# The next expert's first transposes between two experts' bodies, and layer 0's neighbour sums in three segments

## The chip, the cores and the metric

The kernel runs on one core of a Trainium2 chip. A core has five engines with a sequence of instructions each: TensorE (PE in the profile) multiplies matrices and transposes, VectorE (DVE) and ScalarE (ACT) work element by element, GpSimd (POOL) issues the transfers that gather and scatter by an index, and SyncE (SP) issues most other transfers. They wait for each other through semaphores. The metric is the time on the device in microseconds (us): the median over runs of the whole program.

## The reference

The input x has 625 rows (nodes) of 1024 float32 values, and 10,625 edges (src, dst). Two parts are added to it in turn:

```python
deg_inv = 1.0 / maximum(degree(dst), 1)
def sage(h, W_self, W_neigh, b):
    mean = segment_sum(h[src], dst) * deg_inv
    return h @ W_self + mean @ W_neigh + b
x = x + sage(relu(sage(layernorm(x), ...layer 0)), ...layer 1)

n = layernorm(x)
w = softmax(n @ gate_w.T) kept for each row's two largest of 8 experts, else 0
for each expert e:
    g, u = n @ gate_up[e].T          # 1408 values each
    out += w[:, e] * ((silu(g) * u) @ down[e].T)
out += sigmoid(n @ shared_expert_gate_w.T) * (shared expert of 176 values)
x = x + out
```

## The kernel before

**Graph part.** The edges are counted into an adjacency matrix on the chip, so that a neighbour sum is a matrix product. Layer 0's neighbour sums are added to h1T, the transposed hidden rows, in the region "sum0": for each half of the nodes (313 and 312 columns) and for each of 8 chunks of 128 features, PE makes a sum in PSUM bank (4 + c) mod 8 (p_sum), and DVE scales it, adds it to h1T and applies the relu, three instructions. Layer 1 begins with `plain(0, half, wn1, q)` (L955): the products p_y of the first 125 nodes into banks 6 and 7. The products of the other nodes follow, by blocks.

**Experts.** The 8 experts run one after the other. An expert's tokens, at most 512, are gathered by their index into four tiles of 128 rows (rows), transposed by PE into xg (features on the partitions, tokens along the free axis) and multiplied by the gate/up weights wg in 11 chunks; silu and the product with u give ht; the down products by wd follow, each scaled by the token's weight gw into ys, and POOL scatters ys onto the output with an add.

The number of tokens of an expert is known only while the kernel runs. The code of an expert therefore is a region with several bodies, one for each number of 64-token units, n = 0 to 7, and every engine branches into the body that fits (Rec.emit, L294: a Switch); PE has further variants for the width. For n up to 2 a body is small: `few` for 128 tokens, with the tokens as the stationary operand, `unit` for 64 left over. Above that it is `many`, with the weights stationary. Ahead of the branch stands a hint (`hint`, L727), which tells the sequencer where it will go. A body ends with a branch to the code behind the region, which is common to all: the hint for the next expert, the copies gw (`weights`, L1307, DVE) and the branch into the next expert's body.

Each body is cut into segments (`k.point()`): three for gate/up (s = 0, 1, 2), then one for each part of the down products. An instruction outside a region, or a DMA issued within it, that needs something of a segment waits for the end of that segment on the engine concerned, since the bodies differ within it. A wait from outside on an earlier instruction of a segment is so a wait on the segment's last one.

**Around the change.** `expand(j, ...)` (L1303) transposes token tile j: for each of two groups of four features' chunks, PE makes four transposes into one PSUM bank and an engine copies the bank into xg; its `engines` name the two that copy, DVE and ACT if nothing is said. `expand(0, ...)` for the next expert stands at the end of the last gate/up segment (L1569), ahead of the down products; tiles 1 to 3 are made at the start of the expert's own body (L1555), copied by ACT. Program order is queue order on each engine. The first expert's tile 0 is made ahead of its region (L1321). In `many` the first chunk of gate/up products is done in two halves over the features, so that its first half needs only the first of the two copies; `few` and `unit` do it in one piece. The gathers of the next expert's rows are issued by POOL after an expert's first gate/up segment. The weights of the next expert are loaded into wg and wd by SP as the products that read them end.

Of the kernel before, what the change touches and what calls it, by code (L numbers as in the profile page):

```python
# [301 lines left out]
def gnn_moe(nc, x, src, dst, w_gnn0, w_gnn1, b0, b1, w_gu, w_down, ws_up, ws_down, out):  # L302
# [203 lines left out]
    def tt(o, a, b, op):  # L506
        return k.op("DVE", lambda h: h.tensor_tensor(o, a, b, op), r=[a, b], w=[o])  # L507
# [382 lines left out]


    k.open("sum0", 2)
    for n, (n0, nn) in enumerate(HALVES):
        for k.cls in range(2):
            for c in range(KD):
                q, o, t = bank("p_sum", (4 + c) % 8)[:, :nn], node_half(c, n), summed[c % 2][:, :nn]
                cols = slice(c * 128, (c + 1) * 128)
                if k.cls:
                    mm(q, [(y0[:, s, cols], at[:, s, n0:n0 + nn]) for s in range(NT)])
                    add(o, q)  # L900
                else:
                    mm(q, [(z[:, s, cols], cb[:, s, n0:n0 + nn]) for s in range(NT) for z in (zh, zm, zl)])
                    tt(t, q, deg_row[:, n0:n0 + nn], ALU.mult)
                    add(o, t)
                ts(o, o, 0.0, None, ALU.max)
        k.cls = None
        k.point()
# [395 lines left out]
    def expand(j, m=128, two=(4, 5), engines=("DVE", "ACT")):  # L1303

        transpose(xg[:, :, j * 128:j * 128 + m], rows[j][:, :D], m, two, "p_xg" if two[0] > 3 else "p_gu", engines)

    def weights(e):  # L1307
        for j in range(NTL):
            copy(gw[:, e % 2, j:j + 1], rows[j][:, D + e:D + e + 1])
# [75 lines left out]
    def gu_bank():  # L1385
        bank_turn[0] = (bank_turn[0] + 1) % 4
        return bank("p_gu", bank_turn[0])

    def gu_banks():
        gu_bank()  # L1390
        b = bank_turn[0]
        gu_bank()
        return b, bank_turn[0]

    def gate(h, q):

        act(h, q[:, :, 0, :], AF.Silu)
        tt(h, h, q[:, :, 1, :], ALU.mult)

    def few(s):  # L1400

        for c in range(4 * s, min(4 * s + 4, FC), 2):
            n = min(2, FC - c)
            q = gu_bank().rearrange("p (c a i) -> p c a i", c=2, a=2)[:, :n]
            mm_all(q.rearrange("p c a i -> p c (a i)"),
                   [(xg[:, i, :128], wg[:, c:c + n, i].rearrange("p c a i -> p c (a i)")) for i in range(KD)])
            gate(hid[:, c:c + n, :], q)

    def few_transpose(s, b, eng):
# [8 lines left out]
        k.op("PE", fn, r=[h, ident], w=[p])  # L1418
        copy(ht[:, 4 * s:4 * s + n, :128], p, eng)

    def side_by_side(jobs):

        def fn(h, m=None):
            for n in range(len(jobs[0][1])):
                for o, pairs in jobs:
                    got = h.matmul(o, *pairs[n], start=n == 0, stop=n == len(pairs) - 1, skip_group_check=True)  # L1426
            return got
        k.op("PE", fn, r=[x for o, pairs in jobs for p in pairs for x in p], w=[o for o, pairs in jobs])

    def unit(s, t0):  # L1430

        q = gu_bank().rearrange("p (c a i) -> p c a i", c=2, a=2)
        x = [xg[:, i, t0:t0 + 64] for i in range(KD)]

        def job(half, to, what):
            return q[64 * half:64 * half + 64][:, to], [(x[i], what(i)) for i in range(KD)]
        c = 4 * s
        if c + 4 <= FC:
            side_by_side([(q[64 * b:64 * b + 64].rearrange("p c a i -> p c (a i)"),
                           [(x[i], wg[:, c + 2 * b:c + 2 * b + 2, i].rearrange("p c a i -> p c (a i)"))  # L1440
                            for i in range(KD)]) for b in range(2)])
            gate(hid_u[:, 2 * s:2 * s + 2, :], q)
        else:

            side_by_side([(q[64 * b:64 * b + 64, 0].rearrange("p a i -> p (a i)"),
                           [(x[i], wg[:, c + b, i].rearrange("p a i -> p (a i)")) for i in range(KD)]) for b in range(2)])
            side_by_side([(q[64 * b:64 * b + 64, 1, 0, :],
                           [(x[i], wg[:, c + 2, i, 1 - b]) for i in range(KD)]) for b in range(2)])
            gate(hid_u[:, 2 * s:2 * s + 1, :], q[:, :1])
            o = hid_u[:64, 2 * s + 1, :]  # L1450
            act(o, q[64:, 1, 0, :], AF.Silu)
            tt(o, o, q[:64, 1, 0, :], ALU.mult)
# [18 lines left out]
    def many(s, m):  # L1471

        for c in range(4 * s, min(4 * s + 4, FC)):
            pp = [bank("p_gu", 2 * (c % 2) + a) for a in range(2)]

            parts = (range(KD // 2), range(KD // 2, KD)) if c == 0 else (range(KD),)
            for some in parts:
                for a in range(2):
                    mm_all(pp[a], [(wg[:, c, i, a, :], xg[:, i, :]) for i in some], True, some is parts[0], some is parts[-1])
            o = ht[:, c, :m]  # L1480
            act(o, pp[0][:, :m], AF.Silu)
            tt(o, o, pp[1][:, :m], ALU.mult)
# [52 lines left out]
    for e in range(NE):  # L1535
        more = e + 1 < NE
        k.open(e, UNITS)

        def transposed(s, n):

            if n > 0:
                few_transpose(s, 4, "ACT")
            if n % 2 == 0:
                unit_transpose(s, 64 * n, 5, "ACT")

        for s in range(SEG):
            for n in range(UNITS):
                k.cls = n
                full, odd = (n + 1) // 2, n % 2 == 0
                small = n < SMALL // 64  # L1550
                if small and full:
                    few(s)
                if s == 0:
                    for j in range(1, full + odd):
                        expand(j, 128 if j < full else 64, ((4, 5), (0, 1), (2, 3))[j - 1], ("ACT", "ACT"))  # L1555
                    if odd:
                        for b in range(2):
                            copy(gs[64 * b:64 * b + 64, :], gw[:64, e % 2, full:full + 1])
                if small:
                    if odd:  # L1560
                        unit(s, 128 * full)
                    if s:
                        transposed(s - 1, n)
                else:
                    many(s, 64 * n + 64)
                if e == s == 0:
                    own_indices(range(HEAD, NE), 7, "ACT")
                if s == SEG - 1 and more:
                    expand(0, two=gu_banks() if small else (2, 3))  # L1569
            k.cls = None  # L1570
            k.point()
            if e == s == 0:
                wd_loads = [load(wd[c], w_down[0, c]) for c in range(FC)]
            if more:
                for c in range(4 * s, min(4 * s + 4, FC)):
                    load_gu(e + 1, c, [wd_loads[DOWN_FIRST]] if c == 0 else ())
                if s == 0:
                    for j in range(NTL):
                        gather(e + 1, j)
        now = []  # L1580


        for j, stages in ((None, (0, 1)), *((j, (0, 1)) for j in range(NTL - 1, 0, -1)), (0, (0,)), (0, (1,))):
            for n in range(UNITS):
                k.cls = n
                full, odd = (n + 1) // 2, n % 2 == 0
                first = n < SMALL // 64 and (j is None or not odd or full == 0)
                between = (lambda: transposed(SEG - 1, n)) if first else None
                if odd and (j is None and full or j == 0 and not full):
                    down_unit(e, 128 * full, between, stages)  # L1590
                elif j is not None and j < full:
                    down(e, j, between, odd, stages)
            k.cls = None
            k.point()
            halves_of = (None,) if more else (0, 1)
            if stages == (0,):
                if more:
                    wd_loads = [load(wd[c], w_down[e + 1, c]) for c in range(CUT)]
                continue
            for half in halves_of:  # L1600
                now.append(scatter(e, j, half))
        k.close()
        scattered = now
        if more:
            hint(e + 1, bodies)
            weights(e + 1)
            if e + 2 == NE:
                for half in range(2):
                    ts(idx_h[:, half, :], idx[:, e + 1, :], 2.0, float(half), ALU.mult, ALU.add)
            wd_loads += [load(wd[c], w_down[e + 1, c]) for c in range(CUT, FC)]  # L1610
# [111 lines left out]
```

## Time and profile before

| what | value |
|---|---|
| runs | 1119.47, 1120.13, 1117.36 us; median 1119.47 |
| the profiled execution | 1116.6 us, span 1114.8 us |
| mean granted TensorE clock | 0.991 |
| PE, busy | 1078.0 us |
| DVE, busy | 289.7 us |
| ACT, busy | 127.5 us |
| POOL, busy | 50.2 us |
| data moved | 186.53 MB, mean 167 GB/s |
| experts' part, first to last gate/up or down product | 407.86 to 1104.7 us |

In a row of the profile's timeline stand the start, the busy time, the engine, the line, the operation, output <- inputs with their shapes, the count, and in brackets how long the engine stood idle before it and what ended that idle time. "issue" is idle time that no wait in the profile explains. An engine's name with a q (DVEq) is its sequencer: it takes the branches and hints, which the busy times leave out. "p_gu", "p_xg" and "p_down" are PSUM banks under the names of their use; the transposes of a token tile appear as L597 with p_gu or p_xg, depending on the bank. The seven experts' boundaries lie at 501.9, 533.0, 736.5, 795.2, 826.3, 940.2 and 1046.8 us.

### The profile page before, as it was taken

To read this page: it belongs to the slowest core of one execution; us is meant where nothing else is said; L and a number is where in the kernel's file an instruction comes from. 1 tells how busy PE (TensorE), PEld (TensorE's weight loads), DVE (VectorE), ACT (ScalarE), POOL (GpSimd) and SP (SyncE) were. 2 spreads that over 40 slices of the span, in tenths; PEclk is the share of its full clock that TensorE was granted. 3 is DMA by queue.
4 is the path that set the end of the run, shared out by engine and by line. 5 is a ranking of instruction groups with operands and counts; after the bars stand their busy time and mean duration, and the time that the engine had idled before them with its cause. 6 is when DMAs were issued, how large, how long until landed. Compare 5 with 4: busy or idle time off the path is not lost.

```text
span 1114.8 us, 10854 instructions
## 1 busy us (share of the span) xinstructions
PE 1078.0 (97%) x4265; PEld 616.8 (55%) x4265; DVE 289.7 (26%) x719; ACT 127.5 (11%) x246; POOL 50.2 (5%) x56
## 2 busy tenths in 40 slices
PE   6999999999999989999899999999989999999996
PEld 3554777444555544544455554445349965995452
DVE  7954556653644350101000000000010000000000
ACT  1122320211000240101100000001010000000010
POOL 0000000000000040001000000100100001000001
PEclk9999999999999999999999999999999999999998
DMA  9600021311042259969933113278799545642601
GB/s 299 250 1 5 1 66 47 152 49 31 1 174 88 74 159 314 362 251 386 403 134 151 76 75 123 38 253 338 271 404 366 226 163 159 231 180 115 215 34 26
DMA packets 40874, 186.53 MB, mean 167 GB/s; under 512 B 6933, under 2 KB 6933, under 8 KB 29300
## 3 DMA queue, kind: packets, MB, share of 16 engines
q1 hardware_dynamic: 34432, 168.18, 39.1%
q0 software_dynamic: 6000, 16.26, 6.3%
q8 instruction: 62, 1.02, 0.4%
q14 instruction: 120, 0.98, 0.3%
q10 hardware_dynamic: 260, 0.09, 0.0%
HBM read 170.51 MB, written 13.99 MB: 165 GB/s over the span
## 4 chain that ended last, share of the span: by engine, by line
PE 93%; DVE 2%; issue 2%; ACT 1%; DMA 1%; SPq 0%; POOL 0%; POOLq 0%; ACTq 0%; DVEq 0%
PE p_gu L547 34%; PE p_down L1493 20%; PE p_y L539 11%; PE p_sum L539 6%; PE p_h L539 5%; PE p_sage L539 5%; PE p_gu L1426 5%; PE p_gs L539 2%; PE p_downs L539 1%; PE pa L656 1%; PE p_gu L597 1%; PE p_tr L597 1%; DVE ln_st L554 1%; DMA rows<-xfw,idx 0%; DMA xa<-in_x_dram 0%
## 5 line engine op out<-in xcount | busy, mean ns | idle before, releaser
L547 PE MATMUL p_gu<-xg,wg 128*128 128x224 f32 (+1 forms) x1056 | 264.5, 414 | 1.2 <-ACT xg L515 1.2
L547 PEld LDWEIGHTS p_gu<-xg,wg 128*128 128x128 f32 x1056 | 202.2, 192 | 62.7 <-issue 60.4
L1493 PE MATMUL p_down<-wd,ht 128*128 128x512 f32 (+1 forms) x616 | 229.5, 594 | 0.0
L1493 PEld LDWEIGHTS p_down<-wd,ht 128*128 128x128 f32 (+1 forms) x616 | 95.0, 175 | 125.0 <-issue 124.8
L507 DVE TENSOR_TENSOR ht<-ht,p_gu 128x256 f32<-128x256 f32 (+3 forms) x63 | 27.5, 437 | 369.2 <-PE p_gu L547 232.7
L547 PE MATMUL p_gu<-wg,xg 128*128 128x512 f32 (+1 forms) x288 | 116.4, 564 | 0.9 <-DVE ht L507 0.6
L547 PEld LDWEIGHTS p_gu<-wg,xg 128*128 128x128 f32 x288 | 55.0, 192 | 59.8 <-issue 57.4
L539 PE MATMUL p_y<-wn,h0T 128*125 128x512 f32 x160 | 72.7, 609 | 1.3 <-ACT h0T L515 1.3
L520 ACT ACTIVATE ht<-p_gu 128x256 f32<-128x256 f32 (+3 forms) x63 | 24.9, 396 | 427.8 <-PE p_gu L547 357.7
L1426 PE MATMUL p_gu<-wg,xg 128*64 128x512 f32 (+2 forms) x384 | 58.3, 461 | 0.5 <-ACT xg L515 0.5
L503 DVE TENSOR_SCALAR ys<-p_down,gw 128x512 f32<-128x512 f32 x10 | 7.5, 751 | 182.6 <-PE p_down L1493 182.6
L539 PE MATMUL p_h<-h0T,ws 128*128 128x313 f32 x192 | 51.1, 426 | 0.0
L539 PEld LDWEIGHTS p_y<-wn,h0T 128*125 128x125 f32 x160 | 29.9, 192 | 37.9 <-issue 35.1
L1360 POOL DMA_INDIRECT out_dram<-ys,idx x13 | 19.9, 1532 | 554.3 <-DVE ys L503 320.2
L539 PEld LDWEIGHTS p_h<-h0T,ws 128*128 128x128 f32 x192 | 36.2, 189 | 14.7 <-issue 0.4
L1426 PEld LDWEIGHTS p_gu<-wg,xg 128*64 128x64 f32 x384 | 25.5, 137 | 32.2 <-issue 28.1
L539 PE MATMUL p_y<-wn,h1T 128*125 128x512 f32 x96 | 41.6, 593 | 1.5 <-DVE h1T L503 1.5
L539 PE MATMUL p_sage<-ws,h1T 128*125 128x512 f32 x96 | 41.9, 592 | 0.0
L503 DVE TENSOR_SCALAR os<-node,src_f 125x640 f16<-125x640 f16 x85 | 33.2, 391 | 2.8 <-PE pa L656 2.8
L539 PEld LDWEIGHTS p_y<-wn,h1T 128*125 128x125 f32 x96 | 18.0, 188 | 24.5 <-issue 22.2
L539 PEld LDWEIGHTS p_sage<-ws,h1T 128*125 128x125 f32 x96 | 17.9, 188 | 22.1 <-issue 21.7
L504 DVE TENSOR_SCALAR od<-node,dmod,dval_i 125x79 bf16<-125x79 f16 x85 | 26.5, 312 | 0.0
(202 smaller groups left out, 775.9 us busy)
## 6 DMA issues: line engine op xcount, KB each, us to landing
wg<-in_w_gu_dram SPq DMA_DIRECT2D x88, 1024.0 KB, 10.8
wd<-in_w_down_dram SPq DMA_DIRECT2D x88, 512.0 KB, 9.0
wn<-in_w_gnn_dram SPq DMA_DIRECT2D x16, 512.0 KB, 13.8
ws<-in_w_gnn_dram SPq DMA_DIRECT2D x16, 512.0 KB, 13.4
xr<-in_x_dram SPq DMA_DIRECT2D x5, 448.0 KB
xfw<-xf SPq DMA_DIRECT2D x5, 448.0 KB
out_dram<-xr SPq DMA_DIRECT2D x5, 448.0 KB
xa<-in_x_dram SPq DMA_DIRECT2D x4, 448.0 KB
```

The costliest lines, as they stand in the source:

```text
L503: return k.op("DVE", lambda h: h.tensor_scalar(o, i, s1, None, op0=op0), r=aps, w=[o])
L504: return k.op("DVE", lambda h: h.tensor_scalar(o, i, s1, s2, op0=op0, op1=op1), r=aps, w=[o])
L507: return k.op("DVE", lambda h: h.tensor_tensor(o, a, b, op), r=[a, b], w=[o])
L520: return k.op("ACT", lambda h: h.activation(o, i, f, **kw), r=aps, w=[o])
L539: k.op("PE", lambda h, a=a, b=b, s=s, e=e: h.matmul(o, a, b, start=s, stop=e, skip_group_check=True), r=[a, b], w=[o])
L547: got = h.matmul(o if m is None else o[:, :m], a, b if m is None else b[:, :m], start=start and n == 0, stop=stop and n == len(pairs) - 1, ...
L554: k.op("DVE", lambda h, part=part, st=st: h.bn_stats(st, part), r=[part], w=[st])
L597: got = h.transpose(pt[:, c, :], i[:n, (4 * g + c) * 128:(4 * g + c + 1) * 128], ident[:n, :n])
L656: k.op("PE", lambda h, s=s: h.matmul(pa[:, s, :], o_s[:, s, :], o_d[:, :DIG], start=c == 0 and s == 0, stop=c == EC - 1 and s == NT - 1, s ...
L1360: h.indirect_dma_start(out=to, out_offset=bass.IndirectOffsetOnAxis(ap=i, axis=0), in_=y, in_offset=None, compute_op=ALU.add).then_inc(s, 16)
L1426: got = h.matmul(o, *pairs[n], start=n == 0, stop=n == len(pairs) - 1, skip_group_check=True)
L1493: got = h.matmul(o[job], *pairs[job][n], start=n == 0, stop=n == FC - 1, skip_group_check=True)
```

## The change

1. The transposes of the next expert's tile 0 and their two copies are taken out of the bodies (where they were between the gate/up and the down products) and stand behind the region, between the next expert's hint and its gw copies. Both copies are DVE's; before, one was DVE's and one ACT's. The banks are 4 and 5. In the large bodies the later tiles change banks for that: tile 1 uses 2 and 3 (before 4 and 5), tile 2 uses 4 and 5 (before 0 and 1), tile 3 stays at 2 and 3.
2. The first chunk of gate/up products is cut into two halves over the features in `few` and `unit` as well (first_chunk).
3. In "sum0" the second half of the nodes is two segments, chunks 0 to 3 and chunks 4 to 7, each with its end.

```diff
-    for n, (n0, nn) in enumerate(HALVES):
+    for n, some in ((0, range(KD)), (1, range(KQ)), (1, range(KQ, KD))):
+        n0, nn = HALVES[n]
         for k.cls in range(2):
-            for c in range(KD):
+            for c in some:
...
-    def gu_banks():
-        gu_bank()
-        b = bank_turn[0]
-        gu_bank()
-        return b, bank_turn[0]
...
+    def first_chunk(c):
+
+        return (range(KD // 2), range(KD // 2, KD)) if c == 0 else (range(KD),)
 
     def few(s):
...
-            mm_all(q.rearrange("p c a i -> p c (a i)"),
-                   [(xg[:, i, :128], wg[:, c:c + n, i].rearrange("p c a i -> p c (a i)")) for i in range(KD)])
+            for some in first_chunk(c):
+                mm_all(q.rearrange("p c a i -> p c (a i)"),
+                       [(xg[:, i, :128], wg[:, c:c + n, i].rearrange("p c a i -> p c (a i)")) for i in some],
+                       False, some[0] == 0, some[-1] == KD - 1)
...
-    def side_by_side(jobs):
+    def side_by_side(jobs, some=range(KD)):
 
         def fn(h, m=None):
-            for n in range(len(jobs[0][1])):
+            for n in some:
...
     def unit(s, t0):
...
+            for some in first_chunk(c):
+                side_by_side(jobs, some)
...
                     for j in range(1, full + odd):
-                        expand(j, 128 if j < full else 64, ((4, 5), (0, 1), (2, 3))[j - 1], ("ACT", "ACT"))
+                        two = (4, 5) if small or j == 2 else (2, 3)
+                        expand(j, 128 if j < full else 64, two, ("ACT", "ACT"))
...
-                if s == SEG - 1 and more:
-                    expand(0, two=gu_banks() if small else (2, 3))
...
         if more:
             hint(e + 1, bodies)
+            expand(0, engines=("DVE", "DVE"))
             weights(e + 1)
```

More of the change, by code (lines that the diff above doesn't have):

```diff
@@ L1427, in fn @@
             return got
-        k.op("PE", fn, r=[x for o, pairs in jobs for p in pairs for x in p], w=[o for o, pairs in jobs])
+        k.op("PE", fn, r=[x for o, pairs in jobs for n in some for x in pairs[n]], w=[o for o, pairs in jobs])
     def unit(s, t0):
@@ L1438, in unit @@
         if c + 4 <= FC:
-            side_by_side([(q[64 * b:64 * b + 64].rearrange("p c a i -> p c (a i)"),
-                           [(x[i], wg[:, c + 2 * b:c + 2 * b + 2, i].rearrange("p c a i -> p c (a i)"))
-                            for i in range(KD)]) for b in range(2)])
+            jobs = [(q[64 * b:64 * b + 64].rearrange("p c a i -> p c (a i)"),
+                     [(x[i], wg[:, c + 2 * b:c + 2 * b + 2, i].rearrange("p c a i -> p c (a i)"))
+                      for i in range(KD)]) for b in range(2)]
+            for some in first_chunk(c):
+                side_by_side(jobs, some)
             gate(hid_u[:, 2 * s:2 * s + 2, :], q)
@@ L1474, in many @@
             pp = [bank("p_gu", 2 * (c % 2) + a) for a in range(2)]
-            parts = (range(KD // 2), range(KD // 2, KD)) if c == 0 else (range(KD),)
-            for some in parts:
+            for some in first_chunk(c):
                 for a in range(2):
-                    mm_all(pp[a], [(wg[:, c, i, a, :], xg[:, i, :]) for i in some], True, some is parts[0], some is parts[-1])
+                    mm_all(pp[a], [(wg[:, c, i, a, :], xg[:, i, :]) for i in some], True, some[0] == 0, some[-1] == KD - 1)
             o = ht[:, c, :m]
```

## The prediction

> **What bounds the kernel now.** I read first the page's busy shares and its chain of work that ended last:
>
> ```profile
> PE 1078.0 (97%) x4265; PEld 616.8 (55%) x4265; DVE 289.7 (26%) x719; ACT 127.5 (11%) x246; POOL 50.2 (5%) x56
> PE 93%; DVE 2%; issue 2%; ACT 1%; DMA 1%; SPq 0%; POOL 0%; POOLq 0%; ACTq 0%; DVEq 0%
> ```
>
> TensorE (PE) sets the time: whatever makes it wait counts in full, and another engine's work counts only where PE waits for it. So the next view is the chain in order of time, at the seven places where one expert's body ends and the next begins:
>
> ```profile
> 521.91 0.87 PE p_gu L597 x8
> ...
> 525.11 7.88 PE p_down L1493 x36
> 532.99 3.98 issue
> 536.97 1.54 PE p_xg L597 x8
> 538.51 2.34 PE p_gu L597 x12
> ...
> 670.04 66.44 PE p_down L1493 x176
> 736.48 27.46 PE p_gu L547 x64
> ```
>
> A body's last down product ends at a time that I call E. At E = 736.48 PE goes from the last down product to the next gate/up product with no gap. The seven E are 501.93, 532.99, 736.48, 795.23, 826.28, 940.21 and 1046.82; the next gate/up product starts after 0, 8.31, 0, 0, 5.49, 1.12 and 0 us (the chain and the timeline). The 8 transposes "p_gu L597" before the down products are the ones that the change moves: 0.87 us of PE for each of 7 experts.
>
> The third view is DVE's timeline and its sequencer's records at the same boundary:
>
> ```profile
> 736.52 0.75 DVE L503 TENSOR_SCALAR ys<-p_down,gw 128x512 f32<-128x512 f32 x1 [18.13 <-PE p_down L1493]
> 742.54 0.34 DVE L516 COPY gw<-rows 128x1 f32<-128x1 f32 x4 [5.27 <-issue]
> ```
> ```profile
> L294 DVEq COMPARE_BRANCH  x2: 53/54/56, 736.5 to 742.9; - x2
> ```
> ```profile
> L727 DVEq MOVE  x3: 36/36/36, 741.9 to 742.3; - x3
> ```
>
> DVE issues its scaling of the last down product at E, then takes the branch out of the body at 736.5. Its next instruction, the first of the branch hint, comes at 741.9: 5.4 us in which it executes nothing. The hint takes some 0.6 us, and the gw copies start at 742.54. Today that lateness is free, as nothing that PE needs soon stands there. The gw copies start at E + 6.71, 6.17, 6.06, 6.20, 6.11, 6.89 and 6.02 at the seven boundaries, whichever body is left.
>
> **The change, part by part.**
>
> *Removed from the bodies.* The 8 transposes of the next expert's first tokens: 7 x 0.87 = -6.1 us on PE. They filled PE while ACT and DVE gated the last chunk. Behind them PE has the last transposes of hid only after two further down chunks (0.86 us or more, "p_down L1493" before "p_ht"), against about 0.75 us for ACT's silu (0.28) and DVE's product (0.29) with their hand-overs, so I put that cover's loss at 0; lost whole it costs at most 0.5 us in the four small bodies. ACT loses one 0.58 us copy in each, off the path.
>
> *Put between the bodies.* In the changed kernel's order DVE has: branch out, hint, two xg copies, gw copies, branch in. PE's 8 transposes come at E, 1.04 us by the timeline, and are done long before DVE comes. DVE's first copy stands where the gw copies stand now, and the row for this tile is 0.69 us ("COPY xg<-p_gu", 692 ns). PE starts about 0.04 us after the copy (as at 831.73 to 831.77 after ACT's). The next gate/up product therefore starts at E plus the gw offsets plus 0.73: 7.44, (6.90), 6.79, 6.93, 6.84, 7.62, 6.75. The second copy comes 0.69 us later, hidden by the new split of the first chunk: four products of 0.43 us, or eight in the large bodies. The cover gone, it is 0.69 us each, 5 in all.
>
> The second boundary leads into the body for 448 tokens, whose later transposes and ACT copies set the start. ACT arrives at E + 4.71 as now; the pair of banks 4 and 5, now the third tile's, is free only when DVE has copied (E + 6.9 and 7.6), so I add 0.6 for each four transposes and 0.6 for each copy, and come to E + 9.2 instead of 8.31. The later starts against now: 7.44 + 0.9 + 6.79 + 6.93 + (6.84 - 5.49) + (7.62 - 1.12) + 6.75 = 36.7. Less 6.1: **+30.6 us**.
>
> *What else is behind DVE's copies.* The gw copies come 1.37 us later, and POOL's next gathers wait for them; they land in 9.2 us (median), the shortest body is 24 us long. DVE enters the next body at about E + 14 instead of E + 12.5 (its branch in takes 4.2 to 6.1 us more); its first product is wanted when the first chunk ends at about E + 13 or later and PE has another pair of banks to fill: 0. SP's loads wait for PE's reads of the down weights, which end at E as before. No DMA moves.
>
> *The clock.* A PE that idles loses clock afterwards. The granted clock (the third figure from the end of a row; the DMA share and GB/s follow it) in stretches of the span, after the 2.6 us wait at 403.5 and after the fifth boundary:
>
> ```profile
> 403.50:406.10 2.60, 0.04 (x2) 0.01 (x1) 0.00 (x0) 0.69 (x1) 1.87 (x2) 1.00 0.88 252
> ...
> 407.80:411.10 3.30, 3.24 (x4) 1.51 (x5) 3.30 (x19) 0.08 (x2) 3.00 (x2) 0.50 0.84 258
> 411.10:414.00 2.90, 2.90 (x8) 1.29 (x7) 1.12 (x10) 0.00 (x0) 2.29 (x3) 1.00 0.99 331
> ```
> ```profile
> 831.00:834.30 3.30, 2.53 (x7) 2.31 (x8) 0.34 (x4) 1.07 (x2) 0.97 (x1) 0.50 1.02 382
> 834.30:837.60 3.30, 3.30 (x11) 2.97 (x10) 0.00 (x0) 0.00 (x0) 0.00 (x0) 0.50 1.03 369
> ```
>
> Half clock lasted 3.3 us after the one and 6.6 after the other, and costs half of that: 1.6 to 3.3 us. Five boundaries that have no long gap now get 5.5 to 5.9 us of idle PE. The rule of the Trainium skill ("TensorE: Matmul & The Clock Gate", Part 1: The HAM clock gate) is that one idle window of some 3.4 us halves the clock, and one busy window of the same length restores it. By the rule taken at its shortest the cost is 5 x 1.7 = 8.5 us; by the rows, where the rest of a begun window comes on top, about 5 us of half clock each, 5 x 2.5 = 12.5. I take **+12**, ends 8 and 16.
>
> *A second rule, against my main term.* The skill ("Runtime: NRT & Kernel Launch", Instruction fetch mechanics) has a taken branch stall only when its target isn't in a window of two pages of 256 instructions. One expert's DVE code is some 130 instructions in the order of instructions, so by that the exit should mostly be free; DVE would then copy at about E + 1.0 (when the 0.75 us scaling ends), PE would start at E + 1.7, and the edit would come to about +7 - 6 = +1 us before any clock loss. The trace has 5.3 to 6.2 us at all seven exits; the DMA engines are fully busy just then (share 1.02 in the row of 831). I go by the trace.
>
> *Layer 0's sums in three segments.*
>
> ```profile
> PE p_y L539 <- DVE h1T L503: 1.5, 1, 1.5
> ```
>
> PE's first p_y product of layer 1 goes to bank 6, last read by the third sum of the second half; today it waits for the end of the whole segment, the relu of the eighth sum (197.83 + 0.32), and starts at 198.21, idle 1.45 us. With the cut, it waits for the fourth sum's relu, four steps of 2.0 us earlier, so -1.45. What comes next late is not DVE's: its three 1.2 us sums from 198.37 stand as they were, the product that needs h1T comes 14 us later, and DVE's next row on the chain (226.05) itself waits 3.43 us for PE. Bounds 0 and -1.45; I take -1.45. In the first expert's first chunk the split also lets PE start on DVE's copy before ACT's: at most -0.3 ("p_gu" waited 0.32 for ACT at 407.86), which I take.
>
> **Sum.** 30.6 + 12 - 1.45 - 0.3 = +41 us on the profiled execution's own 1116.6 us (span 1114.8 and 1.8 around it): 1157.5. The median of the runs is 1119.47, 2.9 above that execution: **1160 us**.
>
> **Rivals.** (a) DVE comes sooner, because its exit fetches in less time than now: the shortest stalls in the trace are ACT's 2.4 us at 727.1 and DVE's 2.8 at 86.4, with quiet DMA. With gw offsets of 3.5 PE starts at E + 4.2: 4 x 4.2 + 3.1 + 0 + 0 - 6.1 = +14, clock +8, sums -1.8: about 1139. For it: the stall varies. Against: the same 2.5 MB of down weights are released at the same E.
> (b) It ends faster or the same: the exit stall is gone and DVE copies at E + 1. Then 4 x 1.7 + 0.6 - 6.1 = +1.3, sums -1.8, and the two entry gaps of PE (3.98 and 3.62), whose hint now runs some 1.7 us ahead of the branch, shrink by up to 1.7 each: 1115 to 1119. It decides where PE starts within about 1.1 us of E on average (6.1 + 1.8 us over seven boundaries). Against it: all seven offsets are above 6.
> (c) Worse: the stall grows to the trace's longest DVE branch (166.8 to 173.2, 6.4 us), some 1 us more at each boundary, and the clock takes its upper end: +7 + 4 and some 2 from lost covers, about 1173.
> That the change doesn't do what it says I rule out: the order of instructions shows the moved transposes.
>
> **How the numbers follow.** The forecast has 0.68 (its own range 1149 to 1170), (a) 0.14, (b) 0.06, (c) 0.12. Leaving out (b), the lower part of (a) and the upper part of (c) gives 1139 to 1173. A change within 0.3% can't be told from none here: faster 0.04, same 0.03 (both from b), slower 0.93.
>
> **What would show it.** Right: in the waits, PE at the next gate/up product on DVE's xg copy, some 5 us at five boundaries; DVE's two xg copies each at E + 6; clock 0.50 for 3 to 7 us after each; "p_gu L597" before the down products gone; p_y's wait of 1.5 gone. Wrong: DVE's copies within 3 us of E, no half clock after the new gaps, or PE held at the boundaries by something other than DVE.

## The result, and the profile after

The changed kernel takes 1161.06 us (median of four runs, 1158.96 to 1163.0) against 1118.41 us; the ratio is 1.0382, 95% interval 1.0354 to 1.041. It is slower by 42.7 us; the profiled execution's span grew by 42.4, from 1114.8 to 1157.2 us.

The page of the changed kernel, the two lines that answer to those of before:

```profile
PE 1093.0 (94%) x4265; PEld 622.5 (54%) x4265; DVE 293.5 (25%) x726; ACT 123.9 (11%) x239; POOL 50.3 (4%) x56
PE 90%; issue 4%; DVE 2%; DMA 2%; SPq 1%; ACT 1%; DVEq 0%; POOL 0%; POOLq 0%; ACTq 0%
```

PE executes as many instructions as before and yet is busy 15 us longer: some of them ran slower. The rest of the loss is idle time. PE's waits, with the total, the number and the longest in us:

```profile
PE p_gu L1427 <- DVE xg L516: 12.6, 2, 6.6
PE p_gu L547 <- DVE xg L516: 11.9, 2, 6.0
...
PE p_gu L597 <- issue: 6.9, 2, 3.7
PE p_gu L547 <- issue: 5.3, 1, 5.3
...
PE p_down L1494 <- DVE ht L507: 1.2, 2, 0.6
```

The first two lines are new: at the four boundaries into small bodies the next expert's first gate/up product waits for DVE's copy of xg. The fourth line is the same wait at the sixth boundary, where its cause isn't named: PE starts 0.79 us after the start of DVE's first copy there, and 0.75 at the four. The third line is PE's own way into the two large bodies that follow a small one (7.6 us before, under p_xg). "p_y L539 <- DVE h1T" is gone from the list. The last line is new too, and will matter below.

The boundary shown of before at 736.48 is now at 744.27. PE's and DVE's timeline:

```profile
744.11 1.04 PE L597 MATMUL p_xg<-ident,rows 128*128 128x128 f32 x8
744.31 0.75 DVE L503 TENSOR_SCALAR ys<-p_down,gw 128x512 f32<-128x512 f32 x1 [18.13 <-PE p_down L1494]
750.40 1.29 DVE L516 COPY xg<-p_xg 128x512 f32<-128x512 f32 x2 [5.34 <-issue]
751.15 9.30 PE L547 MATMUL p_gu<-wg,xg 128*128 128x512 f32 x15 [6.00 <-DVE xg L516]
751.61 0.32 DVE L516 COPY gw<-rows 128x1 f32<-128x1 f32 x4
```

The transposes come at E and are done within 1.04 us. DVE scales the last down product at E as well, and then executes nothing for 5.34 us. Its sequencer's records fill that time:

```profile
L294 DVEq COMPARE_BRANCH  x1: 56/56/56, 744.3 to 744.3; - x1
```
```profile
L727 DVEq MOVE  x3: 36/36/36, 749.8 to 750.2; - x3
```

The branch out of the body is issued at 744.3, and the first instruction behind it, of the hint, comes at 749.8, 5.46 us later; the hint takes the last 0.6 us. Only then does DVE copy, and PE goes on 6.9 us after E instead of at once.

The granted clock (third figure from the end of a row) at this boundary, in the stretches of PE's wait and of the next body's first products:

```profile
748.00:751.20 3.20, 0.05 (x1) 0.06 (x1) 0.80 (x2) 0.00 (x0) 0.00 (x0) 0.75 1.00 356
751.00:754.40 3.40, 3.25 (x4) 1.51 (x5) 0.93 (x6) 0.00 (x0) 1.01 (x1) 0.50 1.06 278
754.40:757.80 3.40, 3.40 (x7) 1.33 (x6) 0.00 (x0) 0.00 (x0) 0.00 (x0) 0.70 1.02 394
757.80:761.00 3.20, 3.20 (x9) 1.43 (x8) 0.00 (x0) 0.09 (x1) 0.00 (x0) 1.00 0.71 285
```

The clock is halved towards the end of the wait and stays so until about 756.5. The price: 4 and 7 products are counted in the first two busy stretches, against 9 in the last.

Where the 42.4 us are, from the chain and the timelines of both kernels:

| stretch | before | after | difference |
|---|---|---|---|
| start to the first gate/up product | 407.86 | 406.61 | -1.25 |
| first expert's body | 94.08 | 92.14 | -1.94 |
| the seven stretches from E to the next gate/up product | 14.46 | 51.97 | +37.5 |
| bodies of experts 2 to 8 | 588.31 | 596.83 | +8.5 |
| from the last down product to the end | 10.11 | 9.63 | -0.5 |

The seven stretches are now 6.83, 10.06, 6.87, 7.51, 6.83, 7.09 and 6.78 us.

### The profile page after: what moved, and what is told of

Same layout as the page of the kernel before. It is cut to its first block, busy times and chain, and to the rows that moved or that the text cites. A ratio compares the mean times of both kernels' runs of the same rounds, so it can differ in the third digit from the quotient of the medians.

```text
span 1157.2 us, 10857 instructions
## 1 busy us (share of the span) xinstructions
PE 1093.0 (94%) x4265; PEld 622.5 (54%) x4265; DVE 293.5 (25%) x726; ACT 123.9 (11%) x239; POOL 50.3 (4%) x56
## 3 DMA queue, kind: packets, MB, share of 16 engines
q8 instruction: 62, 1.02, 0.4%
## 4 chain that ended last, share of the span: by engine, by line
PE 90%; issue 4%; DVE 2%; DMA 2%; SPq 1%; ACT 1%; DVEq 0%; POOL 0%; POOLq 0%; ACTq 0%
PE p_gu L547 33%; PE p_down L1494 20%; PE p_y L539 10%; PE p_sum L539 6%; PE p_gu L1427 5%; PE p_h L539 5%; PE p_sage L539 5%; PE p_gs L539 2%; DMA xa<-in_x_dram 1%; PE p_downs L539 1%; PE pa L656 1%; PE p_tr L597 0%; PE p_xg L597 0%; SPq L488 0%; DMA rows<-xfw,idx 0%
## 5 line engine op out<-in xcount | busy, mean ns | idle before, releaser
L547 PE MATMUL p_gu<-xg,wg 128*128 128x224 f32 (+1 forms) x1056 | 267.2, 417 | 6.1 <-issue 5.3
L1494 PE MATMUL p_down<-wd,ht 128*128 128x512 f32 (+1 forms) x616 | 229.7, 594 | 1.2 <-DVE ht L507 1.2
L1494 PEld LDWEIGHTS p_down<-wd,ht 128*128 128x128 f32 (+1 forms) x616 | 95.0, 175 | 127.4 <-issue 125.3
L507 DVE TENSOR_TENSOR ht<-ht,p_gu 128x256 f32<-128x256 f32 (+3 forms) x63 | 27.5, 437 | 413.7 <-PE p_gu L547 248.1
L547 PE MATMUL p_gu<-wg,xg 128*128 128x512 f32 (+1 forms) x288 | 119.9, 577 | 12.5 <-DVE xg L516 11.9
L1427 PE MATMUL p_gu<-wg,xg 128*64 128x512 f32 (+2 forms) x384 | 63.4, 490 | 12.8 <-DVE xg L516 12.6
L539 PE MATMUL p_y<-wn,h0T 128*125 128x512 f32 x160 | 73.2, 613 | 1.3 <-ACT h0T L515 1.3
L539 PE MATMUL p_h<-h0T,ws 128*128 128x313 f32 x192 | 51.1, 426 | 0.0
L539 PEld LDWEIGHTS p_y<-wn,h0T 128*125 128x125 f32 x160 | 30.2, 193 | 38.2 <-issue 35.2
L539 PEld LDWEIGHTS p_h<-h0T,ws 128*128 128x128 f32 x192 | 36.2, 189 | 14.7 <-issue 0.5
L539 PE MATMUL p_sage<-ws,h1T 128*125 128x512 f32 x96 | 41.9, 592 | 0.0
L539 PE MATMUL p_y<-wn,h1T 128*125 128x512 f32 x96 | 41.5, 592 | 0.0
L539 PEld LDWEIGHTS p_y<-wn,h1T 128*125 128x125 f32 x96 | 18.0, 188 | 22.7 <-issue 22.2
L539 PEld LDWEIGHTS p_sage<-ws,h1T 128*125 128x125 f32 x96 | 18.0, 188 | 22.1 <-issue 21.7
L539 PE MATMUL p_gs<-wus,xfT 128*125 128x361 f32 x80 | 25.2, 467 | 0.4 <-DVE xfT L516 0.4
```

What stands on the lines that cost most here:

```text
L539: k.op("PE", lambda h, a=a, b=b, s=s, e=e: h.matmul(o, a, b, start=s, stop=e, skip_group_check=True), r=[a, b], w=[o])
L547: got = h.matmul(o if m is None else o[:, :m], a, b if m is None else b[:, :m], start=start and n == 0, stop=stop and n == len(pairs) - 1, ...
L1494: got = h.matmul(o[job], *pairs[job][n], start=n == 0, stop=n == FC - 1, skip_group_check=True)
```

## Experiments

The theory is that PE waits for DVE because DVE's last instruction in a body can't be issued before E and the branch behind it stalls for over 5 us. Its rivals are that the place costs by itself, whoever copies, and that the clock, not the wait, is the loss or costs nothing. E is again the end of a body's last down product. Each ratio is to the kernel before as it ran beside the experiment; its medians there lie between 1117.06 and 1117.96 us.

**The same place, ahead of the branch.** The transposes and DVE's copies become the last instructions of the body:

```diff
                 elif j is not None and j < full:
                     down(e, j, between, odd, stages)
+                if stages == (1,) and more:
+                    expand(0, engines=("DVE", "DVE"))
...
-            expand(0, engines=("DVE", "DVE"))
```

> The transposes and both DVE copies come at the same place on PE, right behind the last down product, but as the last instructions of the body, ahead of DVE's branch out. If DVE's branch out is what PE waits for, DVE copies right behind its 0.75 us scaling, at E + 1.0 and E + 1.7 (the first product now waits for the segment's end, so for both), PE goes on at E + 2.4 at the five boundaries that had no gap or 1.1 us, and nearly all of the loss is gone: 1124, with up to 3 us of half clock on top. If the place is what costs (transposes and copies behind the last down product, whoever's branch), it stays near 1161.

Measured: 1128.32 us, ratio 1.009 (1.0074 to 1.0106); three quarters of the loss are gone. The third boundary, PE and DVE:

```profile
737.52 1.04 PE L597 MATMUL p_xg<-ident,rows 128*128 128x128 f32 x8
740.76 1.52 PE L547 MATMUL p_gu<-wg,xg 128*128 128x512 f32 x3 [2.21 <-issue]
...
738.39 1.28 DVE L516 COPY xg<-p_xg 128x512 f32<-128x512 f32 x2
```

DVE copies 0.71 us after E (737.68) instead of 6.13. The place isn't what costs. At the four boundaries into small bodies PE goes on at E + 2.04 where a small body is left; where a large one is left, as here, at E + 3.05 and 3.08, 1.1 us beyond the end of DVE's second copy. There it is PE's own branch into the next body, issued at 734.6, that takes 5.87 us: with the transposes inside the body PE leaves it later, and the hint is only 0.4 us ahead of the branch. This second branch I had not reckoned with. At the sixth boundary it takes 5.89 us and PE goes on at E + 4.47; at the three boundaries together that is 3.4 us more than the E + 2.4 expected.

**Who copies.** Both copies given to ACT:

```diff
-            expand(0, engines=("DVE", "DVE"))
+            expand(0, engines=("ACT", "ACT"))
```

> The changed kernel with both copies given to ACT, which leaves its body 5 to 9 us before E. If the lateness of DVE's branch is the cause, PE goes on at E + 1.2 at the four boundaries into small bodies, but ACT then enters the large bodies late (its branch in took 2.8 and 6.5 us), where it has to copy the later tiles: about E + 5, E + 9 and E + 12.5. Sum about 1118 + 10, and 2 to 5 us of half clock: 1130. If it isn't DVE in particular, PE waits at all seven as now: 1161.

Measured: 1125.63 us, ratio 1.0071 (1.0056 to 1.0085). The same boundary, PE and then ACT:

```profile
736.86 2.41 PE L547 MATMUL p_gu<-wg,xg 128*128 128x512 f32 x5 [0.24 <-ACT xg L515]
```
```profile
736.22 1.07 ACT L515 COPY xg<-p_xg 128x512 f32<-128x512 f32 x2 [9.14 <-PE p_xg L597]
```

PE goes on at E + 1.1 at all four boundaries into small bodies. ACT, whose last instruction in the body ended 5.4 to 8.7 us ahead of E, has its branch behind it. Into the large bodies PE now starts at E + 8.76, 7.14 and 6.95, as ACT enters late for the later tiles; about 12.5, 9 and 5 had been expected. Of the boundaries that had no half clock in the kernel before, only the sixth has it here.

**Whose last instruction is at E.** DVE scales the first half of the down products, ACT the last, and in the part for 64 left-over tokens ACT scales both; the last expert keeps its own order:

```diff
-                if b == 0 and e == NE - 1:
+                if b == 0 or e < NE - 1:
...
-            act(y[:, :BANK], q[0], AF.Copy, scale=w)
+            if e < NE - 1:
+                ts(y[:, :BANK], q[0], w, None, ALU.mult)
...
-            ts(y[:, BANK:], q[1], w, None, ALU.mult)
+            if e < NE - 1:
+                act(y[:, BANK:], q[1], AF.Copy, scale=w)
...
```

> The changed kernel with the two scalings of the down products exchanged: DVE scales the first half (4.7 us before E), ACT the second, the last of the body; in the 64-token part ACT scales both. If the engine whose last instruction is at E is the late one, DVE is now early and PE goes on at about E + 2 at the four boundaries into small bodies with no half clock, while ACT is late for the later tiles of the large bodies, about E + 7, E + 13 and E + 17: about 1147. If DVE's lateness has nothing to do with when its last instruction can be issued, its copies stay at E + 6: 1161.

Measured: 1142.72 us, ratio 1.0232 (1.0208 to 1.0255). Two boundaries, into a small body (DVE, then PE) and into a large one:

```profile
740.97 1.29 DVE L516 COPY xg<-p_xg 128x512 f32<-128x512 f32 x2 [9.13 <-PE p_xg L597]
```
```profile
741.72 2.84 PE L547 MATMUL p_gu<-wg,xg 128*128 128x512 f32 x6 [0.35 <-DVE xg L516]
```
```profile
951.64 0.69 ACT L520 ACTIVATE ys<-p_down,gw 128x512 f32<-128x512 f32 x1 [18.15 <-PE p_down L1494]
952.07 1.29 DVE L516 COPY xg<-p_xg 128x512 f32<-128x512 f32 x2 [9.13 <-PE p_xg L597]
...
963.89 1.07 ACT L515 COPY xg<-p_gu 128x512 f32<-128x512 f32 x2 [11.56 <-issue]
964.52 1.86 PE L547 MATMUL p_gu<-xg,wg 128*128 128x224 f32 x4 [11.18 <-ACT xg L515]
```

The same DVE copies behind the same branch now come 0.48 us after E and PE goes on at E + 1.2: DVE's last instruction in the body was issued 5.5 to 9.5 us ahead of E, and its branch is hidden. The lateness has moved to ACT, with 11.56 us of "issue" for two branches and the hint, and PE goes on only 12 to 14 us after E where it needs ACT's copies. The engine that is late is the one whose last instruction in the body is at E. That settles the theory.

**Why the branch takes over 5 us.** First the five loads of down weights that SP issues at E were held back until DVE's last gw copy (`weights` now returns it):

```diff
-            weights(e + 1)
+            last = weights(e + 1)
...
-            wd_loads += [load(wd[c], w_down[e + 1, c]) for c in range(CUT, FC)]
+            wd_loads += [load(wd[c], w_down[e + 1, c], after=[last]) for c in range(CUT, FC)]
```

> The changed kernel with the five loads of down weights that SP issues at E held back until DVE's gw copies. If DVE's branch out is slow because its instructions are fetched behind these 2.5 MB, its stall falls from 5.4 us to 2.5 to 3 at the boundaries that leave the large bodies (the third, sixth and seventh), where little else is moving, and the copies come at E + 3.5 there: 1150 to 1153. If the load has no part in it, the copies stay at E + 6: 1161.

Measured: 1161.83 us, ratio 1.0398 (1.0374 to 1.0422), and DVE's copies at E + 6.1 to 7.0. That looks like a no. But the DMA share (second figure from the end) behind E at 744.69 shows that the run didn't do what it was for:

```profile
744.70:748.00 3.30, 0.87 (x8) 0.63 (x6) 0.75 (x1) 0.00 (x0) 1.54 (x1) 1.00 1.02 412
```

The six loads issued before E (740.4 to 743.7) were still moving. So all eleven were held back:

```diff
-                if more:
-                    wd_loads = [load(wd[c], w_down[e + 1, c]) for c in range(CUT)]
...
-            wd_loads += [load(wd[c], w_down[e + 1, c]) for c in range(CUT, FC)]
+            wd_loads = [load(wd[c], w_down[e + 1, c], after=[last]) for c in range(FC)]
```

> The changed kernel with all eleven loads of down weights held back until DVE's gw copies. In the run that held back five of them the DMA engines were still fully busy for some 4 us behind E with the first six, so it didn't tell. Now little moves at the boundaries that leave the large bodies. If the branch's instructions wait for that traffic, DVE's copies come at E + 3.5 there instead of E + 6.0 to 6.3: three boundaries, 1150 to 1154. If not, they stay at E + 6, and the time is 1161, or more where the loads come too late.

Measured: 1138.72 us, ratio 1.0213 (1.0184 to 1.0243), 22 us faster than the changed kernel. The third boundary (E = 740.64), the stretch behind E and DVE's timeline:

```profile
740.70:744.00 3.30, 0.81 (x8) 0.57 (x6) 0.73 (x1) 0.00 (x0) 1.54 (x1) 1.00 0.01 2
```
```profile
740.68 0.75 DVE L503 TENSOR_SCALAR ys<-p_down,gw 128x512 f32<-128x512 f32 x1 [18.13 <-PE p_down L1495]
744.25 1.29 DVE L516 COPY xg<-p_xg 128x512 f32<-128x512 f32 x2 [2.81 <-issue]
```

With the DMA engines idle (share 0.01) the same branch lets DVE on 2.81 us after the scaling instead of 5.34. DVE copies at E + 3.45 to 3.71 at five boundaries; more than the three expected, since the two that leave a body of 192 or 128 tokens were quiet too. At the two that leave the 64-token bodies gate/up weights still stream (share 1.01 and 1.02), and the copies stay at E + 6.1 and 6.2. So about half of the branch's stall, 5.46 us from branch to hint, goes when the weight loads are out of the way (2.94).

The trace also shows what comes between. The profile counts the transfers of each DMA queue, and queue 14 is of the kind "instruction". In the changed kernel it has no packet between DVE's branch at 744.3 and 747.8, and one from there to the hint (747.80 to 749.80). With the loads held back it has the only packet of all queues between 741.60 and the hint at 743.6. The two rows, in this order:

```profile
q14 instruction: 1, 0.01, 1.0%
```
```profile
q14 instruction: 1, 0.01, 1.7%
```

In the first run the packet, of 8 KB, begins 3.57 us behind the branch, in the second 0.98; it takes 0.31 and 0.55 us, and the hint's first instruction follows 1.6 and 1.4 us after its end. It is so at every boundary: the last packet of this queue ahead of the hint begins 3.4 to 4.2 us behind the branch in the changed kernel, 1.0 to 1.3 at the five quiet boundaries of this run, and the hint follows 1.4 to 1.6 us after it. The difference between the two stalls is thus when the packet begins: an instruction fetch that comes later beside the weight loads. Other engines' packets use the queue too, so that this one is DVE's is read from the times; what fills the 1.0 us ahead of it at idle DMA engines, and the 1.4 us behind it, stays open.

**The clock.** 11 products that nobody reads, on PE behind the transposes, into a bank that the next body overwrites:

```diff
+    def fill():
+        o, i = bank("p_gu", 0), rows[0][:, :BANK]
...
+            for _ in range(11):
+                got = h.matmul(o, ident, i, start=True, stop=True, skip_group_check=True)
...
             expand(0, engines=("DVE", "DVE"))
+            fill()
```

> The changed kernel with 11 further products of 128 x 512 on PE behind the transposes at each boundary, into a bank that the next body overwrites, some 4.7 us that lie within the wait for DVE. The starts of the next bodies stay at E + 6.8 to 7.5. If the half clock after the idle stretch costs what the bodies' lengths show (12 to 14 us), this is 1148 though PE does more. If the half clock isn't on the path it stays at 1161; if the wait isn't DVE's, it is 5 x 4.7 us longer, about 1185.

Measured: 1169.63 us, ratio 1.0467 (1.0452 to 1.0482). None of the three numbers: a float32 product of this size is two passes of 0.43 us, and the 11 took 9.6 us, not 4.7.

```profile
747.74 1.04 PE L597 MATMUL p_xg<-ident,rows 128*128 128x128 f32 x8
748.61 9.61 PE L1317 MATMUL p_gu<-rows,ident 128*128 128x512 f32 x22
758.06 1.45 PE L547 MATMUL p_gu<-wg,xg 128*128 128x512 f32 x3
```

So PE itself was late, at E + 10.2 and more, and the wait for DVE was gone. The run tells the clock's price all the same: behind the first expert's start the granted clock is 1.00 at every boundary, and the bodies of experts 2 to 8 take 581.9 us together against 596.8 in the changed kernel, the same instructions. The half clock costs 14.9 us. With five products (the edit against the run with 11):

```diff
-            for _ in range(11):
+            for _ in range(5):
```

> The changed kernel with 5 further products of 128 x 512 on PE at each boundary instead of 11. In the run with 11 they took 9.6 us, as a float32 product is two passes of 0.43 us, twice what had been reckoned, and held up PE itself. Five take 4.4 us and end at E + 5.4, ahead of DVE's copy. If the half clock costs what the bodies' lengths show against that run (596.8 less 581.9, 15 us), this is 1161 - 15 = 1146, with seven times 4.4 us more of work on PE. If the half clock costs nothing, it is 1161.

Measured: 1147.51 us, ratio 1.0268 (1.0252 to 1.0284), 13.5 us less than the changed kernel with 30 us more of products on PE. In the profiled execution, which at 1152.31 us is the slowest of the four, three boundaries still had 3.4 us of half clock, each after 2.4 to 2.9 us of idle PE, so the gain isn't the whole 14.9.

**The split of the first chunk.** The first chunk in one piece again, in `few` and in `unit`, so that PE waits for DVE's second copy too:

```diff
-            for some in first_chunk(c):
+            for some in (range(KD),):
```

> The changed kernel with the first chunk of few and unit in one piece again. PE then waits for DVE's second copy too, 0.69 us more at each of the four boundaries into small bodies: 1161 + 2.8 = 1163.8. If that copy is hidden anyway it stays at 1161.

Measured: 1164.18 us, ratio 1.042 (1.0398 to 1.0442). The difference to the changed kernel is 3.1 us where 2.8 was expected. The changed kernel's own four runs lie up to 2.1 us from their median, so the time alone hardly shows it; the trace does, as PE starts 1.34 us after DVE's first copy at these boundaries instead of 0.75.

**What is left without the move.** The transposes and their banks as in the kernel before, the rest of the change kept; and the three segments alone (the first edit shown of the change):

```diff
+                if s == SEG - 1 and more:
+                    expand(0, two=gu_banks() if small else (2, 3))
...
-            expand(0, engines=("DVE", "DVE"))
```

> The changed kernel with the transposes and their two copies (DVE and ACT) back in the bodies; layer 0's sums in three segments and the split of the first chunk stay. If the whole loss is the move, this is the kernel before less 1.45 us (p_y no longer waits for DVE) and at most 0.3 us: 1116.7 against 1118.4, and PE's waits show no p_y on h1T. If the saved wait only comes back later in the graph part, it is 1118.4. If the split of the first chunk costs something by itself, it is above 1119.

> The kernel before with layer 0's sums in three segments and nothing else. The saved wait is 1.45 us: 0.9987 of the time before. If it comes back later in the graph part, 1.0000. If the better part of the gain of the run with the transposes left in the bodies (0.9975) is this part, 0.9975.

Measured: 1113.98 us, ratio 0.9975 (0.9964 to 0.9986), for the first; 1115.42 us, ratio 0.999 (0.9979 to 1.0001), for the second. The first is 3 us faster than the kernel before, so the whole loss is the move. The three segments alone agree with the 1.45 us expected, 0.9987, and can't be told from nothing by the medians; but the wait for h1T is gone from PE's list, and in this run p_y follows p_sum at once:

```profile
195.71 0.30 PE L539 MATMUL p_sum<-cb,zl 125*128 125x312 bf16 x1
195.84 1.88 PE L539 MATMUL p_y<-wn,h1T 128*125 128x512 f32 x4
```

Most of the spread between runs of one kernel goes with their mean granted clock (for the kernel before, 0.986 with 1119.4 us and 0.993 with 1114.0). An estimate from the times and clocks of all these runs, a straight line with one slope, gives at a clock of 0.990 some 1116.7 us before, 1115.1 with the segments alone and 1114.2 with the split as well. So the segments' gain, 1.6 us with some 0.5 either way, does stand out. Of the last 1.0 us I know 0.3; the rest is open.

## Why the prediction was right

1160 was forecast and 1161.06 measured. The mechanism was right; that the number is within 1.1 us is partly luck. The profiled execution lost 42.4 us where the terms add up to 41, and the 2.9 us added from there to the median came out as 2.1. By its own steps:

*The starts of the next products*, +36.7: measured +37.5. The offsets of DVE's copy were taken from where the gw copies stood, and the copy came at E + 6.04 to 6.77. One by one they differ by up to 0.6 us (the first and sixth boundary earlier, the fourth later); in the sum that cancels, which is luck. That DVE's branch causes the lateness is shown by three runs that leave the transposes behind the last down product (copies ahead of the branch, by ACT, or by a DVE whose last instruction is earlier), each of which brings PE's start at the boundaries into small bodies from E + 6.8 to 7.5 down to E + 1.1 to 3.1. The second boundary, worked out at E + 9.2, was 10.06.

*Removed transposes*, -6.1: this is the term that was mis-sized. In the run with 11 products, which has no half clock in them, the bodies of experts 2 to 5 are shorter than before by 0.87 us each (31.12 to 30.25, 195.18 to 194.31, 58.91 to 58.04, 31.12 to 30.25). That of expert 7 isn't: 105.50 in both. Nor is that of expert 6: 108.44 before, of which 6.0 us at half clock account for some 3, and 105.50 there. These are the large bodies for 240 tokens; their down products wait for the last chunk's ht, "p_down L1494 <- DVE ht L507: 1.2, 2" in the waits, and the transposes had covered that. The prediction put the loss of this cover at 0 and looked for it in the small bodies only. The term is about -4.4, with 0.87 for the first expert too. That body's -1.94 is this, 0.3 for the split (PE's wait at its first gate/up products falls from 0.49 to 0.21 us), and some 0.8 that the prediction didn't reckon with: a stretch of 3.4 us of half clock lies almost whole in the body before, and only 1.6 us of it after.

*The clock*, +12, ends 8 and 16: 14.9 us in the bodies of experts 2 to 8 of the changed kernel by the run with 11 products, of which the kernel before had 2.9 already in the sixth expert's body (108.44 against 105.5): +12.0. The rows were the better guide than the rule taken at its shortest (8.5): the half clock lasted 6.8 us at six boundaries and 10.2 at one, of which 3.0 to 5.3 us fell on the next body.

*The segments*, -1.45: the wait is gone, and the estimate at equal clock is 1.6 us.

*The rule against the row.* By the rule of the Trainium skill on taken branches ("Runtime: NRT & Kernel Launch", Instruction fetch mechanics), that one stalls for a fetch when its target is outside the current two pages of instructions, DVE's exit should have been mostly free, as the prediction reads it, and the edit would have come to about +1 us before the clock. Five boundaries with a wait of 5.3 to 6.6 us on DVE decide for the row. With a packet of the instruction queue behind each of the seven exits, in the kernel before as well, what didn't hold is that their target needs no fetch. The 130 instructions that it was judged by are also too few: in the program as built DVE has 225 to 234 from one expert's entry branch to the next, over all eight bodies. Rival (a), a stall of 2.4 to 2.8 us with quiet DMA, was rejected since the same loads are released at the same E; the run that holds them back is that rival in its mechanism. That it took 1138.7 us where the rival had said about 1139 is partly luck: two boundaries kept the long stall, and the clock cost some 5 us (589.5 us for the bodies of experts 2 to 8, less the 581.9 without half clock and the 2.9 of before), not 8.

## What to carry to other kernels

Work put between two runtime-chosen bodies runs only after its engine has left the first one: read from the sequencer's branch records when each engine leaves, and give the work to an engine whose last instruction is well before the end, or keep it ahead of the branch. A lateness that costs nothing today is a stall for whatever is queued behind it tomorrow. And count a wait on TensorE together with the half clock after it: here the waits were 37.5 us and the clock another 12.

## What the runs showed of the hardware

- From DVE's branch out of a body to its next instruction it was 5.3 to 6.2 us beside DMA engines at share 1.0 (both kernels, all seven boundaries), and 2.8 to 3.0 us beside idle ones (0.01 to 0.04, five boundaries of the run that holds all loads back). An 8 KB packet of the instruction queue comes in between, and it is the packet's beginning that moves.
- PE's branch into the next body took, at the third boundary, 5.87 us where the hint was 0.4 us ahead of it (copies ahead of the branch), 3.96 us at 2.6 us (the changed kernel, 737.5 to 740.1) and 0.29 us at 9.5 us (11 products). Idle DMA engines did not make up for a late hint: 3.48 us at 2.7 us (all loads held back). In these runs a hint is worth what stands between it and its branch.
- The stretches of half clock at the boundaries last one to four times 3.41 us (3.4, 6.8 and 10.2 in the changed kernel, 13.7 where ACT scales last), and 2.4 to 2.9 us of idle PE were enough to bring one about in the run with five products; the 2.2 us at the third boundary with the copies ahead of the branch were not.
